# Block 0's queries and keys stored once, a bias product and three pieces of work moved in a float32 transformer layer

## The chip, the core and the metric

The kernel runs on one core of a Trainium2 chip. The metric is the time of one execution on the device in microseconds, lower is better. A core has five engines that each run their own instructions in order: PE (matrix products), DVE (vectors), ACT (activation functions), POOL (general, slower), and SP, which here only issues DMA transfers. Transfers issued from SP, ACT or POOL are carried out by the core's 16 DMA engines. Engines wait for one another by semaphores.

## The reference

The input is 4096 tokens of 256 features, in float32. The layer is a causal attention with 16 heads of 16 features, followed by a feed-forward part with three gated or Gelu layers, each with a residual and a normalization on both sides:

```python
h = _layernorm(x)
q, k, v = split(h @ w_attn + b_attn)            # 16 heads of 16
logits = einsum('bhqd,bhkd->bhqk', q, k) * 16 ** -0.5
out = softmax(where(causal, logits, -inf)) @ v
x = x + _layernorm(out @ w_proj + b_proj)
h = silu(_tlin(_layernorm(x), w1)) * _tlin(_layernorm(x), w2)
h = gelu(_tlin(gelu(_tlin(h, h1)), h2))
x = x + _layernorm(_tlin(h, w3))
```

`_tlin` is a product with a matrix of -1, 0 and 1 times a scale per output. The attention is the first two thirds of the time, and the change lies at its beginning.

## The kernel before, in words

**Blocks and groups.** Tokens are worked in 8 blocks of 512 (`QB`). For block `j` the queries of the block meet the keys of blocks 0 to `j`, four heads at a time (a group `g`; 4 groups of 4 heads). The pair (j, g) is an item; 32 items run one after the other.

[...]

**Where the halves go.** `features(j, s, c, engine)` makes queries or keys (`s`) of block `j` for eight heads (`c` is 0 or 1): a product on PE into one PSUM bank (`pk` or `pq`), an ACT copy with the bias (`full`), a cast to `hi` and a subtraction to `lo` on `engine`, and then stores to a scratch tensor `halves_of[s, j]` in DRAM (L513, L545 to L551). It has the shape [16 heads, 2, 2, 16 features, 512], and each half is stored twice, so that a store counts 8 heads x 16 features x 512 numbers on the DRAM side. `hi` goes out from SP, `lo` of blocks 0 and 1 from POOL. `full`, `hi` and `lo` have one buffer for keys and one for queries.

**Reading back.** `load_rows` (L554) reads two heads as one tile of 128 rows x 512 (256 KB) with one transfer from SP. `queries(j, g)` loads two such tiles into a pool of two buffers per tag, `keys(n, c)` two tiles for item `n` and key block `c`, into a ring of 16. Every item reads its keys anew, those of block 0 (`c = 0`) too.

**A score unit.** `SharedUnit.products` (L843) multiplies keys by queries into a [128, 2, 512] PSUM tile, `maximum` (L852) takes its largest value on DVE, and `finish` (L859) writes the exponential of it with a shift per block, on ACT; on the diagonal POOL sets entries to zero (L866). `Values.step` multiplies the exponentials by the values on PE (L930). `steps(j)` lists the units of an item: 8j + 5.

**The order of work.** All engines follow the order in which Python records the instructions. `prep(j)` is a generator that normalizes block `j`, transposes it (`pt`), calls `features` four times and makes the values (`pv`); each `yield` ends a piece. A `Background` holds such generators and takes pieces between score units: `even` runs at most one PE piece of one job per call, `step` one piece of the first job, `finish(name)` steps until that job is gone. `project(j)` is the output projection of a finished block, `halve_weights` stores rounded weights for the second part, and `norm_block` starts the second part.

**The opening** (L1115 to L1132). Both `prep(0)` and `prep(1)` run up to their first PE piece, so both blocks are normalized: block 0 by DVE, block 1 by POOL. Then `biases()` (L1102) scales the query bias on DVE and, on PE, multiplies the value bias by the projection (`pb`, L1106), to be added to the projection's bias `bp`. Then `prep(0)` runs until queries and keys of heads 0 to 7 are stored, items 0 and 1 have their queries and keys loaded from SP, `prep(0)` runs to its end, and the score loop begins with `prep(1)` as its background.

Of the kernel before, what the change touches and what calls it, by code (L numbers as in the profile page):

```python
# [10 lines left out]
F32 = mybir.dt.float32  # L11
F32R = mybir.dt.float32r
AF = mybir.ActivationFunctionType
ALU = mybir.AluOpType
# [3 lines left out]
P = 128  # L18
QB = 512
# [98 lines left out]
def sandwich_kernel(  # L118
# [35 lines left out]
    scratch = ctx.enter_context(  # L154
        tc.tile_pool(name="scratch", bufs=1, space=bass.MemoryType.DRAM)
    )
# [199 lines left out]
    def norm_block(j, room, done, early=None):  # L356

        if early is None:
            xb[j] = load_block(0, x1[j])
            for _ in range(3):  # L360
                yield True
        else:
            xb[j] = early
        xj = xb[j]
        mv = stat.tile([P, NT, 2], F32, tag="mv", name=f"mvf_{j}")
        for t in range(NT):
            layernorm_stats(xj[:, t, :], mv, t)
            yield True
        rstd = layernorm_rstd(mv)
        xh = room.tokens(j)  # L370
        for t in range(NT):
            normalize(xh[:, t, :], xj[:, t, :], mv, rstd, t)
        yield True
        if early is not None:
            yield True
        pts = room.banks(f"ptf_{j}")
        for c in range(DC):
            for t in range(NT):
                nc.tensor.transpose(
                    pts[c][:, t * P : (t + 1) * P], xh[:, t, c * P : (c + 1) * P], ident  # L380
                )
        done(pts)
        yield True
# [20 lines left out]
    def attention(shared):  # L404
# [8 lines left out]
        with ExitStack() as actx:  # L413
# [61 lines left out]
            def constants():  # L475
# [35 lines left out]


            halves_of = {  # L513
                (s, j): scratch.tile([H, 2, 2, HD, QB], F32, tag=f"{s}_{j}", name=f"{s}_{j}")
                for s in "kq"
                for j in range(NB)
            }
# [1 line left out]
            def features(j, s, c, engine):  # L519

                i = "qk".index(s)
                ps = room.bank(f"p{s}_{j}_{c}")
                for d in range(DC):
                    yield room.within(d)
                    nc.tensor.matmul(  # L525
                        ps,
                        lhsT=wqk[d][:, i * D + c * P : i * D + (c + 1) * P],
                        rhs=xTs[j][:, d, :],
                        start=(d == 0),
                        stop=(d == DC - 1),  # L530
                    )
                lent.append(True)
                full = piece(f"full{i}", f"full{s}_{j}_{c}")
                nc.scalar.activation(
                    full,
                    ps,
                    AF.Identity,
                    bias=bqk[:, i * DC + c : i * DC + c + 1],
                    scale=1.0 if i else SCALE,
                )  # L540
                hi = piece(f"hi{i}", f"hi{s}_{j}_{c}")
                engine.tensor_copy(hi.bitcast(F32R), full)
                lo = piece(f"lo{i}", f"lo{s}_{j}_{c}")
                engine.tensor_tensor(lo.bitcast(F32R), full, hi.bitcast(F32R), ALU.subtract)
                for half, part in enumerate((hi, lo)):  # L545
                    for d in range(2):
                        at = (d, half) if i else (half, d)
                        queue = nc.gpsimd if shared and j < 2 and half else nc.sync
                        queue.dma_start(
                            out=halves_of[s, j][8 * c : 8 * (c + 1), at[0], at[1]], in_=part  # L550
                        )  # L551
                stored.add((s, j, c))

            def load_rows(tag, name, key, j, h):  # L554

                t = (piece if key == "k" else query)(tag, name, F32R)
                nc.sync.dma_start(
                    out=t.bitcast(F32),
                    in_=halves_of[key, j][h : h + 2].rearrange("h a b d n -> (h a b d) n"),
                )  # L560
                return t

            def query(tag, name, dtype):
# [10 lines left out]
            RING = 2 * NB  # L574
            kT, asked = {}, [0]

            def keys(n, c):

                for pr in range(2):
                    kT[n, c, pr] = load_rows(  # L580
                        f"k{asked[0] % RING}_{pr}", f"k{n}_{c}_{pr}", "k", c, 4 * (n % G) + 2 * pr
                    )
                asked[0] += 1

# [515 lines left out]
            issued = now = 0  # L1100

            def biases():  # L1102
                nc.vector.tensor_scalar(bqk[:, 0:DC], bqk[:, 0:DC], SCALE, None, ALU.mult)
                ps = two_banks("pb")[:, 0, 0:D]
                for c in range(DC):
                    nc.tensor.matmul(  # L1106
                        ps,
                        lhsT=bv[:, c : c + 1].to_broadcast([P, P]),
                        rhs=wp[:, c, :],
                        start=(c == 0),  # L1110
                        stop=(c == DC - 1),
                    )
                nc.vector.tensor_tensor(bp, bp, ps, ALU.add)

            works = [prep(0, nc.vector), prep(1, nc.gpsimd)]  # L1115
            for work in works:
                while bg.piece(work) != Background.PE:
                    pass
            biases()
            while ("q", 0, 0) not in stored:  # L1120
                bg.piece(works[0])
            for n in range(2):
                queries(*items[n])
                keys(*chunks[n])
            while bg.piece(works[0]) is not False:
                pass
            if shared:
                bg.add(("prep", 1), works[1], PREP)
                bg.work[0][3] = Background.PE
            else:  # L1130
                while bg.piece(works[1]) is not False:
                    pass  # L1132
            mxs = {}
            for n, (j, g) in enumerate(items) if shared else ():
                if g == 0:
                    bg.finish(("prep", j))
                if g == G - 1 and j + 1 < NB:
                    while ("q", j + 1, DC - 1) not in stored:
                        bg.step()
                if n + 1 < len(items) and items[n + 1] not in qT:  # L1140
                    queries(*items[n + 1])
                if g == 0:
                    mxs[j] = top.tile([P, G * width(j)], F32, tag="mx", name=f"mx_{j}")
                    columns = iter(mxs[j][:, i : i + 1] for i in range(G * width(j)))
                if (j, g) == (NB - 2, G - 1):
                    for key in ("w1", "w2"):
                        W[key] = weight_pieces(key, TAGS[key])
                        load_pieces(rounded[key], W[key])
                if (j, g) == (NB - 1, G - 2):
                    for _ in halving:  # L1150
                        pass
                    bg.add(("norm", 0), norm_block(0, room, first_features), NORM)
                if (j, g) == (NB - 1, G - 1):
                    W["h1"] = weight_pieces("h1", TAGS["h1"])
                    load_pieces(rounded["h1"], W["h1"])
                for p, (shapes, parts) in enumerate(steps(j)):
                    ask(n, p)
                    if (g, p) == (1, 2) and j + 2 < NB:
                        bg.add(("prep", j + 2), prep(j + 2), PREP)
                    if (g, p) == (0, 2) and j:  # L1160
                        rise_of(j - 1, mxs[j - 1], f"rise_{j}")
                    units = [SharedUnit(j, g, f"{p}_{i}", at) for i, at in enumerate(shapes)]
                    for unit in units:
                        unit.products()
                        values.step(now)
                        now += 1
                        unit.maximum()
                        if n or p:
                            unit.finish()
                    if not n and not p:  # L1170
                        nc.vector.tensor_reduce(run[:, 0:1], mxs[0][:, 0:2], AX.X, ALU.max)
                        spread(run[:, 0:1], 0)
                        for unit in units:
                            unit.finish()
                    values.add(j, g, parts, [unit.e for unit in units], now - 1)
                    if j < 2 or p < NT * j:
                        bg.even(1 + j // 2 - j // 6)
                    if j > 0 and p % 4 == 2 and p < NT * j:
                        next(halving, None)
                if g == G - 2 and j + 1 < NB:  # L1180
                    next_shift(j)
# [326 lines left out]
```

## Time and profile before

| | us |
|---|---|
| median of 3 runs | 2053.32 (2049.60 to 2054.11) |
| the profiled execution | 2048.42 |
| its span in the profile | 2046.5 |
| busy in the span: PE, DVE, ACT, POOL | 1825.3, 1609.8, 1399.2, 552.2 |
| last exponential of the attention ends | 1375.6 |

A profile of one execution gives each instruction's start and length on its engine. The "chain of waits" follows the work that ended last back to the start: at each step to what released it. A line such as `72.14 8.13 DMA k<-k` in it says: from 72.14 us on, 8.13 us were spent waiting for a transfer that writes `k` (the tile) from `k` (the scratch tensor). In a table of windows each row is a stretch of time with every engine's busy time in it, PE's granted clock as a share of full speed, the mean busy share of the 16 DMA engines and what they moved in GB/s. SP's issues in the opening, from its timeline (start, length, line, transfer):

```profile
20.48 1.39 SPq L549 DMA_DIRECT2D k<-hik  x2
23.24 2.60 SPq L549 DMA_DIRECT2D q<-hiq  x2
33.79 0.84 SPq L557 DMA_DIRECT2D q<-q  x2
34.81 0.91 SPq L557 DMA_DIRECT2D k<-k  x2
35.76 0.95 SPq L557 DMA_DIRECT2D q<-q  x2
36.75 1.59 SPq L557 DMA_DIRECT2D k<-k  x2
```

Between 25.84 and 33.79 SP issued nothing: its next instruction loads queries, and they were not all stored yet.

### The profile page before, as it was taken

What the parts mean: (1) busy time and instruction counts of PE and PEld (TensorE: products, weight loads), DVE (VectorE), ACT (ScalarE), POOL (GpSimd) and SP (SyncE); (2) the same over time, 40 slices, a digit from 0 to 9 for tenths busy, and PEclk for the clock granted to TensorE, in tenths of its full rate; (3) what the DMA queues carried; (4) which work ended last, traced back from release to release, by engine and by line L of the source; (5) the groups of instructions that cost most, each with busy time, mean ns of one, the idle gap of its engine ahead of it and who ended that gap; (6) DMA issues with size and microseconds to landing.
All of it is one profiled execution on the core that took longest, in us unless ns stands there. A gap on an engine that the chain in (4) does not pass through costs nothing.

```text
span 2046.5 us, 28401 instructions
## 1 busy us (share of the span) xinstructions
PE 1825.3 (89%) x10518; PEld 932.5 (46%) x10518; DVE 1609.8 (79%) x1894; ACT 1399.2 (68%) x1598; POOL 552.2 (27%) x871
## 2 busy tenths in 40 slices
PE   4799989988888888888888887889999999999997
PEld 2333332322322322223222222228888888888886
DVE  3689998998999999999999999985546456465453
ACT  2699999999999999999999998982212222222221
POOL 3264545434435335333333110000120000000000
PEclk8899999999999999999999998999999999999999
DMA  6756645444235333553234213103100000000000
GB/s 168 229 179 219 191 133 180 147 154 159 98 131 183 116 103 124 161 163 115 76 136 156 98 44 101 63 9 114 53 11 21 15 7 21 1 21 21 1 11 15
DMA packets 134909, 202.09 MB, mean 99 GB/s; under 512 B 16064, under 2 KB 60736, under 8 KB 134752
## 3 DMA queue, kind: packets, MB, share of 16 engines
q1 hardware_dynamic: 130496, 194.56, 29.3%
q0 software_dynamic: 2480, 4.35, 1.0%
q8 instruction: 87, 1.43, 0.3%
q10 hardware_dynamic: 1776, 1.18, 0.3%
q14 instruction: 70, 0.57, 0.1%
HBM read 137.91 MB, written 62.13 MB: 98 GB/s over the span
## 4 chain that ended last, share of the span: by engine, by line
PE 46%; ACT 21%; DVE 19%; issue 6%; DMA 4%; POOL 2%; SPq 1%; ACTq 0%; POOLq 0%; DVEq 0%
PE z L1358 21%; ACT e_s L859 19%; DVE mx L852 18%; PE av L930 7%; PE s L843 7%; PE za L1358 3%; PE zb L1358 2%; PE pyf L1440 2%; DMA k<-k 1%; PE py L314 1%; PE pk L525 1%; PE pv L650 1%; PE pq L525 1%; ACT junk L211 1%; DMA q<-hiq 0%
## 5 line engine op out<-in xcount | busy, mean ns | idle before, releaser
L852 DVE TENSOR_REDUCE mx<-s 128x1 f32<-128x1024 f32 x1056 | 1219.8, 1217 | 72.1 <-PE s L843 66.6
L859 ACT ACTIVATE e_s<-s,shift 128x1024 f32<-128x1024 f32 x1056 | 1153.6, 1117 | 104.9 <-DVE mx L852 81.9
L843 PE MATMUL s<-q,k 64*128 64x512 f32 (+3 forms) x2304 | 517.7, 468 | 161.2 <-ACT e_s L859 144.7
L930 PE MATMUL av<-e_s,v 128*32 128x512 f32 (+2 forms) x4576 | 572.8, 575 | 7.9 <-POOL e_s L866 5.7
L843 PEld LDWEIGHTS s<-q,k 64*128 64x128 f32 x2304 | 208.9, 185 | 752.9 <-ACT e_s L859 652.2
L1425 ACT ACTIVATE fb<-z,sh 128x512 f32<-128x512 f32 x128 | 88.1, 689 | 364.8 <-PE z L1358 340.2
L1358 PE MATMUL z<-hb_0l,h 128*128 128x512 f32 x512 | 199.5, 390 | 0.0
L1358 PE MATMUL z<-hb_0h,h 128*128 128x512 f32 x512 | 199.5, 390 | 0.0
L866 POOL TENSOR_SCALAR_AFFINE_SELECT e_s<-e_s 128x256 f32<-128x256 f32 (+1 forms) x224 | 94.7, 440 | 337.4 <-ACT e_s L859 337.4
L233 POOL TENSOR_TENSOR rstd<-ve,neghalf 128x4 f32<-128x4 f32 (+1 forms) x22 | 20.8, 944 | 608.8 <-DVE ve L231 603.0
L930 PEld LDWEIGHTS av<-e_s,v 128*32 128x32 f32 x4576 | 97.2, 109 | 151.5 <-issue 116.1
L1325 DVE CAST hb_1h<-fb 128x512 fp32r<-128x512 f32 x64 | 27.4, 428 | 155.7 <-ACT fb L1425 155.7
L1402 ACT ACTIVATE sl<-za,s 128x512 f32<-128x512 f32 x64 | 44.0, 690 | 120.4 <-PE za L1358 60.9
L1325 DVE CAST hb_0h<-fb 128x512 fp32r<-128x512 f32 x64 | 28.1, 440 | 99.6 <-ACT fb L1425 99.6
L1358 PEld LDWEIGHTS z<-hb_0h,h 128*128 128x128 f32 x512 | 96.1, 188 | 20.0
L1358 PEld LDWEIGHTS z<-hb_0l,h 128*128 128x128 f32 x512 | 96.2, 188 | 19.8
L1011 POOL TENSOR_SCALAR wc<-wc 128x256 f32<-128x256 f32 x88 | 75.8, 861 | 7.8
L1010 POOL TENSOR_TENSOR wc<-wc,wh 128x256 f32<-128x256 f32 x88 | 64.3, 730 | 7.2
L1012 POOL TENSOR_TENSOR fit<-fit,wc 128x256 f32<-128x256 f32 x88 | 64.2, 730 | 7.3
L1009 POOL CAST wh<-wc 128x256 fp32r<-128x256 f32 x88 | 35.0, 397 | 108.4 <-DMA wc<-in_h_t_dram 75.9
L1440 PE MATMUL pyf<-w,hb_1l 128*128 128x256 f32 x256 | 61.8, 284 | 0.0
L1440 PE MATMUL pyf<-w,hb_1h 128*128 128x256 f32 x256 | 61.7, 283 | 0.0
(257 smaller groups left out, 1970.3 us busy)
## 6 DMA issues: line engine op xcount, KB each, us to landing
k<-k SPq DMA_DIRECT2D x288, 256.0 KB
q<-q SPq DMA_DIRECT2D x64, 256.0 KB
x<-in_x_dram SPq DMA_DIRECT2D x16, 512.0 KB
k<-hik SPq DMA_DIRECT2D x32, 256.0 KB
q<-hiq SPq DMA_DIRECT2D x32, 256.0 KB
wc<-in_h_t_dram SPq DMA_DIRECT2D x64, 128.0 KB
r_h<-wh SPq DMA_DIRECT2D x64, 128.0 KB
h<-r_h SPq DMA_DIRECT2D x32, 256.0 KB
```

What stands on the lines that cost most here:

```text
L843: nc.tensor.matmul(self.both[:, i, col : col + n], lhsT=kT[G * j + g, c, pr][r, tt * P : (tt + 1) * P], rhs=qT[j, g][pr][r, QB - n :], sta ...
L852: nc.vector.tensor_reduce(next(columns), self.both.rearrange("p a n -> p (a n)"), AX.X, ALU.max)
L859: nc.scalar.activation(e, self.both, AF.Exp, bias=shifts[j])
L866: nc.gpsimd.affine_select(out=here, in_=here, compare_op=ALU.is_ge, fill=0.0, base=0, pattern=[[0, here.shape[1]], [1, P]], channel_multip ...
L930: nc.tensor.matmul(self.av[h * HW : (h + 1) * HW, QB - n :], lhsT=vb[kt // NT][:, kt % NT, o : o + HW], rhs=of(es, h), start=(kt == 0 or k ...
L1010: nc.gpsimd.tensor_tensor(w, w, hi, ALU.subtract)
L1011: nc.gpsimd.tensor_scalar(w, w, 0.0, None, ALU.is_equal)
L1012: nc.gpsimd.tensor_tensor(fit, fit, w, ALU.mult)
L1325: nc.vector.tensor_copy(hi, full)
L1358: nc.tensor.matmul(ps, lhsT=w[c], rhs=single(part[:, c, :]), start=(c == 0 and i == 0), stop=(c == kc - 1 and i == parts - 1),)
L1425: nc.scalar.activation(h, z, AF.Gelu, scale=sc[:, oc : oc + 1])
L1440: nc.tensor.matmul(ps[:, 0:D], lhsT=single(part[:, c, t * P : (t + 1) * P]), rhs=(w3_r if halves else w3_sb)[:, c, :], start=(c == 0 and i ...
```

## The change

1. Block 0's scratch tensors keep each half once: `[16, 16, 2, 512]` for keys, `[16, 2, 16, 512]` for queries. For block 0 `features` issues one store per half, not two. Blocks 1 to 7 still store each half twice, with the last two of the small axes exchanged.
2. `load_rows` of block 0 reads each half twice: a query tile with one transfer whose source repeats each row, a key tile with two transfers (one head each), whose source repeats the head's 32 rows.
3. `keys` and `load_rows` take the queue to issue from. Item 0's keys are issued from POOL, all others from SP as before.
4. The bias product `pb` and its addition to `bp` stand behind the whole of `prep(0)`; the scaling of the query bias stays where it was.
5. Ahead of the score loop `prep(1)` is stepped until the keys of its heads 0 to 7 are stored: two transposes and one pass of `features`.
6. In item (7, 2) the background first finishes `project` of block 6, and then adds `norm_block`.

```diff
             halves_of = {
-                (s, j): scratch.tile([H, 2, 2, HD, QB], F32, tag=f"{s}_{j}", name=f"{s}_{j}")
+                (s, j): scratch.tile(
+                    [H, 2, HD, 2, QB] if j else [H, HD, 2, QB] if s == "k" else [H, 2, HD, QB],
+                    F32, tag=f"{s}_{j}", name=f"{s}_{j}",
+                )
...
                 for half, part in enumerate((hi, lo)):
-                    for d in range(2):
+                    queue = nc.gpsimd if shared and j < 2 and half else nc.sync
+                    kept = halves_of[s, j][8 * c : 8 * (c + 1)]
+                    for d in range(2) if j else ():
                         at = (d, half) if i else (half, d)
-                        queue = nc.gpsimd if shared and j < 2 and half else nc.sync
-                        queue.dma_start(
-                            out=halves_of[s, j][8 * c : 8 * (c + 1), at[0], at[1]], in_=part
-                        )
+                        queue.dma_start(out=kept[:, at[0], :, at[1]], in_=part)
+                    if not j:
+                        queue.dma_start(out=kept[:, :, half] if i else kept[:, half], in_=part)
                 stored.add((s, j, c))
-            def load_rows(tag, name, key, j, h):
+            def load_rows(tag, name, key, j, h, queue=nc.sync):
                 t = (piece if key == "k" else query)(tag, name, F32R)
-                nc.sync.dma_start(
-                    out=t.bitcast(F32),
-                    in_=halves_of[key, j][h : h + 2].rearrange("h a b d n -> (h a b d) n"),
-                )
+                to, part = t.bitcast(F32), halves_of[key, j][h : h + 2]
+                if j:
+                    queue.dma_start(out=to, in_=part.rearrange("h a d b n -> (h a d b) n"))
+                elif key == "k":
+                    for i in range(2):
+                        rows = part[i : i + 1].rearrange("u d b n -> u (d b) n")
+                        queue.dma_start(
+                            out=to[i * P // 2 : (i + 1) * P // 2],
+                            in_=rows.broadcast_to([2, 2 * HD, QB]),
+                        )
+                else:
+                    rows = part.rearrange("h a (d u) n -> (h a d) u n", u=1)
+                    queue.dma_start(out=to, in_=rows.broadcast_to([P // 2, 2, QB]))
                 return t
...
             def biases():
-                nc.vector.tensor_scalar(bqk[:, 0:DC], bqk[:, 0:DC], SCALE, None, ALU.mult)
                 ps = two_banks("pb")[:, 0, 0:D]
...
-            biases()
+            nc.vector.tensor_scalar(bqk[:, 0:DC], bqk[:, 0:DC], SCALE, None, ALU.mult)
             while ("q", 0, 0) not in stored:
                 bg.piece(works[0])
             for n in range(2):
                 queries(*items[n])
-                keys(*chunks[n])
+                keys(*chunks[n], nc.sync if n or not shared else nc.gpsimd)
             while bg.piece(works[0]) is not False:
                 pass
+            biases()
             if shared:
                 bg.add(("prep", 1), works[1], PREP)
                 bg.work[0][3] = Background.PE
+                while ("k", 1, 0) not in stored:
+                    bg.step()
...
                 if (j, g) == (NB - 1, G - 2):
                     for _ in halving:
                         pass
+                    bg.finish(("project", NB - 2))
                     bg.add(("norm", 0), norm_block(0, room, first_features), NORM)
```

More of the change, by code (lines that the diff above doesn't have):

```diff
@@ L513, in attention @@
             halves_of = {
-                (s, j): scratch.tile([H, 2, 2, HD, QB], F32, tag=f"{s}_{j}", name=f"{s}_{j}")
+                (s, j): scratch.tile(
+                    [H, 2, HD, 2, QB] if j else [H, HD, 2, QB] if s == "k" else [H, 2, HD, QB],
+                    F32,
+                    tag=f"{s}_{j}",
+                    name=f"{s}_{j}",
+                )
                 for s in "kq"
@@ L545, in features @@
                 for half, part in enumerate((hi, lo)):
-                    for d in range(2):
+                    queue = nc.gpsimd if shared and j < 2 and half else nc.sync
+                    kept = halves_of[s, j][8 * c : 8 * (c + 1)]
+                    for d in range(2) if j else ():
                         at = (d, half) if i else (half, d)
-                        queue = nc.gpsimd if shared and j < 2 and half else nc.sync
+                        queue.dma_start(out=kept[:, at[0], :, at[1]], in_=part)
+                    if not j:
+                        queue.dma_start(out=kept[:, :, half] if i else kept[:, half], in_=part)
+                stored.add((s, j, c))
+            def load_rows(tag, name, key, j, h, queue=nc.sync):
+                t = (piece if key == "k" else query)(tag, name, F32R)
+                to, part = t.bitcast(F32), halves_of[key, j][h : h + 2]
[4 more added lines that the diff above has]
+                        rows = part[i : i + 1].rearrange("u d b n -> u (d b) n")
                         queue.dma_start(
-                            out=halves_of[s, j][8 * c : 8 * (c + 1), at[0], at[1]], in_=part
-                        )
-                stored.add((s, j, c))
-            def load_rows(tag, name, key, j, h):
-                t = (piece if key == "k" else query)(tag, name, F32R)
-                nc.sync.dma_start(
-                    out=t.bitcast(F32),
-                    in_=halves_of[key, j][h : h + 2].rearrange("h a b d n -> (h a b d) n"),
-                )
+                            out=to[i * P // 2 : (i + 1) * P // 2],
+                            in_=rows.broadcast_to([2, 2 * HD, QB]),
+                        )
+                else:
+                    rows = part.rearrange("h a (d u) n -> (h a d) u n", u=1)
+                    queue.dma_start(out=to, in_=rows.broadcast_to([P // 2, 2, QB]))
                 return t
@@ L575, in attention, with keys @@
             kT, asked = {}, [0]
-            def keys(n, c):
+            def keys(n, c, queue=nc.sync):
                 for pr in range(2):
                     kT[n, c, pr] = load_rows(
-                        f"k{asked[0] % RING}_{pr}", f"k{n}_{c}_{pr}", "k", c, 4 * (n % G) + 2 * pr
+                        f"k{asked[0] % RING}_{pr}",
+                        f"k{n}_{c}_{pr}",
+                        "k",
+                        c,
+                        4 * (n % G) + 2 * pr,
+                        queue,
                     )
```

## The prediction

> **What bounds the kernel now.** I read the chain of waits first, then the groups of instructions by line, then the chain in order of time for the opening, and last short windows with the share of the DMA engines.
>
> The chain and the two costliest groups:
>
> ```profile
> PE 46%; ACT 21%; DVE 19%; issue 6%; DMA 4%; POOL 2%; SPq 1%; ACTq 0%; POOLq 0%; DVEq 0%
> L852 DVE TENSOR_REDUCE mx<-s 128x1 f32<-128x1024 f32 x1056 | 1219.8, 1217 | 72.1 <-PE s L843 66.6
> L859 ACT ACTIVATE e_s<-s,shift 128x1024 f32<-128x1024 f32 x1056 | 1153.6, 1117 | 104.9 <-DVE mx L852 81.9
> ```
>
> Until about 1380 us each of 1056 score units costs a maximum (1.22 us) and an exponential (1.12 us), side by side; after that PE is the bound. The change touches neither. DMA has only 4% of the chain, nearly all of it in the opening. The same chain in order of time:
>
> ```profile
> 23.86 9.77 DMA q<-hiq
> ...
> 35.21 5.63 DMA k<-k
> ...
> 72.14 8.13 DMA k<-k
> ...
> 81.53 10.63 DMA k<-k
> ```
>
> The first and second waits are block 0's stores and the read back, the third and fourth the keys of group 3 of block 0 and group 0 of block 1. The timeline of ACT and PE says what that costs:
>
> ```profile
> 31.10 2.00 PE L650 MATMUL pv<-wv,xT 128*128 128x256 f32 x8 [0.68 <-ACT v L658]
> 38.98 0.80 PE L843 MATMUL s<-q,k 64*128 64x512 f32 x2 [5.88 <-DMA k<-k]
> 44.42 2.12 ACT L859 ACTIVATE e_s<-s,shift 128x1024 f32<-128x1024 f32 x2 [10.70 <-DVE shift L1040]
> 94.16 2.24 ACT L859 ACTIVATE e_s<-s,shift 128x1024 f32<-128x1024 f32 x2 [1.87 <-DVE mx L852]
> 169.24 2.24 ACT L859 ACTIVATE e_s<-s,shift 128x1024 f32<-128x1024 f32 x2 [0.90 <-DVE mx L852]
> ```
>
> The last three are the first exponentials of blocks 0, 1 and 2. Block 0's four groups hold 4 x 5 units, some 35 us of work at the 8.9 us that a group took, but 49.7 us lie between the first two. So the opening has about 14 us of waiting; that is all a change here can win.
>
> Now the windows with the DMA share (before the last figure, which is GB/s):
>
> ```profile
> core 0: us, PE busy (x) PEld busy (x) DVE busy (x) ACT busy (x) POOL busy (x), PEclk, DMA share, GB/s
> 45.00:47.00 2.00, 1.38 (x8) 0.84 (x8) 1.32 (x2) 2.00 (x4) 0.81 (x2) 0.50 0.52 203
> 51.00:53.00 2.00, 2.00 (x4) 0.50 (x5) 0.00 (x0) 0.32 (x1) 0.63 (x1) 0.50 0.95 342
> 90.00:92.00 2.00, 1.26 (x6) 0.76 (x4) 0.00 (x0) 1.81 (x5) 0.87 (x3) 1.00 0.97 363
> 109.00:111.00 2.00, 1.49 (x20) 0.73 (x20) 2.00 (x3) 1.97 (x3) 1.58 (x5) 1.00 0.48 176
> ```
>
> In 51 to 53 and 90 to 92 only loads of whole 128-row tiles ran: all 16 engines busy. In 45 to 47 only stores of hik and hiq ran, whose DRAM side counts 8 heads x 16 x 512; in 109 to 111 mostly oo and xT0lo, whose DRAM side counts 8 x 16 x 512 too: half of the engines. So a transfer runs on no more engines than the outermost count of either side allows. Per busy engine the four windows give 22.5 to 24.4 GB/s; I use 23.4. Then 256 KB cost an engine 0.70 us over 16 engines and 1.40 us over 8.
>
> **The change part by part.** The bias product leaves the front: pb held PE from 12.37 to 14.42 waiting for wp, while block 0's tokens were normalized at 10.80 (9.42 + 1.38). So the transposes may start some 3.3 us sooner and the first hi store goes out at 17.2 instead of 20.48. The first lo store gains less: POOL still normalizes block 1 until 19.22 (14.38 + 4.84), so 19.3 instead of 21.48.
>
> The stores of block 0 fall from 16 to 8, 4 MB to 2 MB. Those of k now count 128 rows on both sides, so by the row they run on 16 engines. With one hi and one lo store each, hiq and loq land near 25.5 (issue near 20.7, then the 4 to 5 us that the first hik needed: 20.48 to 26.1 for two). The queries can be loaded then, not at 33.79: 8 us sooner.
>
> Three pieces of block 1 and pb stand ahead of the first scores on PE. With the rows' durations: second pv ends at 29.7, pb 31.7, pt 32.8, copy, pt 34.1, copy, pk 36.7. So the first scores run at 36.7, 2.3 us sooner, even if their keys lie ready at 30. The pieces aren't lost: block 0's own 12 steps have four PE pieces fewer to carry. What is queued behind them: DVE now has hik and lok of block 1 (0.43 + 0.69) ahead of the first maximum, and hik must wait until the store of block 0's second hik has landed (one buffer).
>
> The last edit (finishing project before norm) moves nothing: in the built order of instructions every engine's rows agree from block 5 on, but for the key loads. In blocks 1 to 4 the background stands one place later. I cost both at nothing; the cover is the maximum of 1.22 us per unit.
>
> Then the reading twice. Queries: 64 rows x 2, outermost counts 64 and 128: 0.70 us as before. Keys: each tile is now two transfers of 128 KB, with 64 rows on the SBUF side and **2 x 32 x 512 on the DRAM side, the 2 a repeat**. No row shows a count of 2. By what 8 does to stores and to loads alike, 2 means two engines: 64 KB each at 23.4 GB/s, 2.80 us per transfer, 11.2 us per group of four, on the same two engines if the choice always starts with the first. The other end is 8 or 16 engines: 0.35 to 0.70 us per transfer, 1.4 to 2.8 per group. I take two, since both kinds of row fell with the count. It holds for every group of every block but the very first, whose four go by POOL.
>
> [...]
>
> Those two engines get, until the keys of block 2's first group are there: block 0's keys for 8 groups, 8 x 11.2 = 89.6; other keys of block 1, 8 x 0.70 = 5.6; queries 18 x 0.70 = 12.6; SP's stores, block 0 4.2, block 1 8 x 1.40, block 2 16 x 1.40, together 37.8; POOL's 12 stores 0 to 16.8, taken as 8.4; 7 outputs 4.9; three x loads 4.2; oo and xT0lo 5.6; weights 2.1. Sum 170.8 us. From the first store at 17 that is 187.8; with 2.1 us for scores and maximum (0.8 + 1.24) block 2's first exponential comes at 190 against 169.24: **+21**. POOL's stores elsewhere: +12. Idle time of the two engines (about 5 us before the first keys, 6 us while SP waits for block 1's hiq) and POOL's stores on them: up to +40. I take the middle, **+26**. In block 2 the two engines get 11.2 + 2.8 + 1.4 + 5.6 + 1.4 + 0.7 + 0.7 + 3.5 = 27.3 us per group against 25.7 that a group took: 0 to +6, kept for the range. From block 3 on it is about 30 against 36 us: hidden, and 62 more issues of 0.45 us on SP lie beside 1200 us of scores.
>
> Span 2046.5 + 26 = 2072.5. The median of the runs, 2053.3, lies 6.8 above that span, so 2079.
>
> **The rivals.** *Spread (faster).* If key loads use 8 or more engines, or a changing pair, the first exponential comes at 42.3 (36.7 + 5.6 for two maxima, shift and block 1's casts) and block 1's at 42.3 + 4 x 8.9 + 3 x 1.5 = 82.4 instead of 94.16: -12, 2041; bounds -17 (no gaps) and -4 (half the gaps stay, with more to carry): 2036 to 2049. For it: there is no row with a count of 2, and the waits of 8.13 and 10.63 us are real. Against: the two halved windows.
>
> [...]
>
> *The jam spreads (far slower).* SP's queue is in order and each half has one buffer: behind a late store wait DVE's casts (block 1) or POOL's (block 2 on), and with them the maxima or the masks. If every group of blocks 0 to 2 loses 5 us more, +60: 2110.
>
> **How the numbers follow.** Two fixed engines 0.61 (own range 2061 to 2099), spread 0.24, hidden 0.08, jam 0.07. Faster or slower by over 0.2% (4 us, about what a measurement of this kernel can tell) follows from the same cases. Slower: 0.61 + 0.07 + 0.02 = 0.70; same 0.06 (hidden, less what falls outside 4 us); faster 0.24. The likeliest gives 2079. The range reaches down into the spread case to 2038 and up to 2100, and leaves out the jam and the best of the spread.
>
> **What would show it.** Right: windows with k<-k alone at a share near 0.13 and 45 to 50 GB/s; a first exponential of block 0 near 47 (hik of block 1 held by a store), of block 1 near 101 and of block 2 near 195; PE s waiting for k<-k 30 us or more in all; blocks 3 to 7 unchanged. Wrong: key loads landing within 4 us at a share near 1, block 1 starting before 85. The stores are right if the wait of 9.77 us for hiq is gone in either case.

## The result and the profile after

| | before | after |
|---|---|---|
| median of 4 runs, us | 2053.72 (2049.60 to 2055.87) | 2122.12 (2119.28 to 2124.76) |
| ratio to before, 95% interval | | 1.0335 (1.0312 to 1.0358) |
| span of the profiled execution | 2046.5 | 2117.5 |
| first exponential of block 0, 1, 2 | 44.42, 94.16, 169.24 | 54.77, 115.67, 210.91 |
| first exponential of block 3, last one's end | 276.25, 1375.6 | 334.82, 1447.6 |

The change made the kernel 3.35% slower. The prediction had the direction and the two slow DMA engines, but said 2079. The chain of waits of after, and the same two groups of instructions:

```profile
PE 44%; ACT 19%; DVE 16%; DMA 10%; issue 6%; SPq 3%; POOL 2%; ACTq 0%; POOLq 0%; DVEq 0%
L872 DVE TENSOR_REDUCE mx<-s 128x1 f32<-128x1024 f32 x1056 | 1220.1, 1215 | 112.2 <-PE s L863 108.3
L879 ACT ACTIVATE e_s<-s,shift 128x1024 f32<-128x1024 f32 x1056 | 1154.9, 1116 | 156.5 <-DVE mx L872 128.2
```

The busy times are those of before within 1.3 us (1219.8 and 1153.6). What grew is the third figure, the idle time ahead of them: 72 to 112 for the maxima, 105 to 157 for the exponentials. DMA went from 4% to 10% of the chain, and SP's own queue from 1% to 3%. So no work was added to the two engines that set the pace; they wait.

Some of SP's issues in the opening, and three windows in which hardly anything but block 0's keys was being read:

```profile
18.77 0.34 SPq L557 DMA_DIRECT2D k<-hik  x1
23.31 0.75 SPq L557 DMA_DIRECT2D q<-hiq  x1
30.85 2.65 SPq L575 DMA_DIRECT2D q<-q  x4
33.61 4.56 SPq L569 DMA_DIRECT2D k<-k  x4
38.27 2.35 SPq L557 DMA_DIRECT2D k<-hik  x1
```

```profile
39.00:41.00 2.00, 0.16 (x2) 0.00 (x0) 0.00 (x0) 0.28 (x1) 0.00 (x0) 1.00 0.13 51
45.00:49.00 4.00, 0.00 (x0) 0.00 (x0) 0.00 (x0) 0.00 (x0) 0.00 (x0) 0.50 0.13 50
117.00:122.00 5.00, 3.59 (x23) 1.36 (x27) 1.39 (x2) 1.45 (x3) 0.00 (x0) 0.57 0.13 49
```

A share of 0.13 is two engines of 16, at 49 to 51 GB/s. In 45 to 49 PE, DVE, ACT and POOL do nothing, and SP issues nothing between 41.36 and 50.40: all five stand still behind two busy DMA engines. The last line of the first fence says what they wait for. This store was issued at 38.27, after four key loads of 33.61 to 38.17. The chain in order of time shows that one and its like (start, length, what):

```profile
24.31 6.53 DMA q<-loq
...
38.27 11.59 DMA k<-hik
...
71.73 15.84 DMA k<-hik
...
103.66 14.70 DMA k<-k
...
124.20 10.70 DMA avd<-av_sb
...
152.88 11.77 DMA x<-in_x_dram
...
219.51 11.62 DMA avd<-av_sb
```

Only some of these are waits for the keys themselves. The others are a store of `hik`, the store of an attention output (`avd`) and a load of tokens (`x`). None of them belongs to block 0's reading, and each took 10 to 16 us (11.59 and 15.84, 10.70 and 11.62, 11.77). That they were late because they stood on SP behind key loads is so far a reading of the order of issue; experiments 4, 6 and 7 test it. What waits for the first `hik` store is on DVE:

```profile
49.95 0.43 DVE L547 CAST hik<-fullk 128x512 fp32r<-128x512 f32 x1 [15.47 <-DMA k<-hik]
```

This cast of block 1 waits for the buffer that the store of 38.27 empties. DVE runs in order, the first maximum is the instruction after next and starts at 51.02, and so the first exponential comes at 54.77.

### The profile page after: what moved, and what is told of

The parts are those of the page before. It is cut to its first block, busy times and chain, and to the rows that moved or that the text cites. A ratio compares the mean times of both kernels' runs of the same rounds, so it can differ in the third digit from the quotient of the medians.

```text
span 2117.5 us, 28458 instructions
## 1 busy us (share of the span) xinstructions
PE 1853.8 (88%) x10518; PEld 939.4 (44%) x10518; DVE 1612.2 (76%) x1894; ACT 1401.9 (66%) x1598; POOL 553.3 (26%) x871
## 4 chain that ended last, share of the span: by engine, by line
PE 44%; ACT 19%; DVE 16%; DMA 10%; issue 6%; SPq 3%; POOL 2%; ACTq 0%; POOLq 0%; DVEq 0%
PE z L1381 20%; ACT e_s L879 17%; DVE mx L872 14%; PE av L950 7%; PE s L863 6%; DMA avd<-av_sb 3%; PE za L1381 2%; PE zb L1381 2%; PE pyf L1463 2%; DMA k<-k 2%; DMA k<-hik 1%; PE py L314 1%; DMA x<-in_x_dram 1%; SPq L569 1%; SPq L565 1%
## 5 line engine op out<-in xcount | busy, mean ns | idle before, releaser
L863 PE MATMUL s<-q,k 64*128 64x512 f32 (+3 forms) x2304 | 527.2, 474 | 196.6 <-ACT e_s L879 163.1
L950 PE MATMUL av<-e_s,v 128*32 128x512 f32 (+2 forms) x4576 | 583.8, 586 | 7.5 <-POOL e_s L886 5.7
L1348 DVE CAST hb_1h<-fb 128x512 fp32r<-128x512 f32 x64 | 27.4, 427 | 155.7 <-ACT fb L1448 155.7
L1029 POOL CAST wh<-wc 128x256 fp32r<-128x256 f32 x88 | 35.0, 397 | 209.1 <-DMA wc<-in_h_t_dram 142.1
```

Source lines behind the costliest of these rows:

```text
L863: nc.tensor.matmul(self.both[:, i, col : col + n], lhsT=kT[G * j + g, c, pr][r, tt * P : (tt + 1) * P], rhs=qT[j, g][pr][r, QB - n :], sta ...
L950: nc.tensor.matmul(self.av[h * HW : (h + 1) * HW, QB - n :], lhsT=vb[kt // NT][:, kt % NT, o : o + HW], rhs=of(es, h), start=(kt == 0 or k ...
L1348: nc.vector.tensor_copy(hi, full)
```

## The experiments

All times are medians; the ratio to the kernel before, run on the same chip, stands with its 95% interval. Experiments 1 to 4, 5 to 8 and 9 to 12 ran on three chips; where two from different chips are compared, it is by these ratios.

**1. Reading with four 32-row transfers in place of two that repeat.** After, with each key tile of block 0 read by four transfers of 32 different rows:

```diff
-                    for i in range(2):
-                        rows = part[i : i + 1].rearrange("u d b n -> u (d b) n")
-                        queue.dma_start(
-                            out=to[i * P // 2 : (i + 1) * P // 2],
-                            in_=rows.broadcast_to([2, 2 * HD, QB]),
-                        )
+                    for i in range(4):
+                        rows = part[i // 2 : i // 2 + 1].rearrange("u d b n -> (u d b) n")
+                        queue.dma_start(out=to[i * 2 * HD : (i + 1) * 2 * HD], in_=rows)
```

> The changed kernel with one edit: a key tile of block 0 is loaded by four transfers of 32 rows, none with a repeated source, in place of two transfers of 64 rows whose source repeats 32 rows twice. Same rows in the same places, stores once as in the changed kernel. Theory (two engines): all of the loss comes from the key loads that run on two engines, so the share of 0.13 is gone, block 1 starts before 90, and the time is 2036 to 2049 (the spread case of the prediction). Rival (order): the moved bias product, the pieces ahead of the scores or the new layout cause the loss; then it stays above 2100. Rival (number of transfers): eight transfers per group instead of four hold up SP; then between 2060 and 2100.

2048.17 us, ratio 0.9979 (0.9966 to 0.9992). Same bytes, twice as many issues, and the whole loss is gone. The first exponentials of blocks 0 and 1 are these:

```profile
45.92 1.11 ACT L876 ACTIVATE e_s<-s,shift 128x1024 f32<-128x1024 f32 x1 [7.88 <-DVE shift L1057]
95.33 1.11 ACT L876 ACTIVATE e_s<-s,shift 128x1024 f32<-128x1024 f32 x1
```

So the repeat as the outermost count is the cause of the loss. But the rival *Spread*, whose case this is, had 42.3 and 82.4 here: without the two engines the change still doesn't win the 12 us that *Spread* named.

**2. Only the moved work.** Before, with its own stores and loads, and the bias product behind `prep(0)`, the three pieces ahead of the scores, and the last edit:

```diff
-            biases()
+            nc.vector.tensor_scalar(bqk[:, 0:DC], bqk[:, 0:DC], SCALE, None, ALU.mult)
...
+            biases()
             if shared:
...
+                while ("k", 1, 0) not in stored:
+                    bg.step()
...
+                    bg.finish(("project", NB - 2))
```

> The kernel before with the moved bias product, the pieces of block 1 ahead of the first scores and the finish of project, but with its own stores and loads. Theory (two engines): no loss; a little gain or none, 2044 to 2056, since block 0's stores still bound the first scores. Rival (order): above 2075.

2049.97 us, 0.9978 (0.9968 to 0.9988): as fast as experiment 1. Storing block 0 once, read well, adds nothing to the moved work. One line of DVE shows that the opening gains nothing, without any two-engine load:

```profile
46.57 0.43 DVE L542 CAST hik<-fullk 128x512 fp32r<-128x512 f32 x1 [11.71 <-DMA k<-hik]
```

The three pieces put block 1's cast ahead of the first maximum, and its buffer is still being stored. The first exponentials of blocks 0 and 2 come at 51.40 and 173.31, later than before (44.42 and 169.24), and the attention ends at 1377.14 (1375.6). So where the 0.2% comes from, this profile doesn't show.

**3. Only the stores and reads of the change.** After, with the bias product, the pieces and the queue of item 0's keys as before:

```diff
+            biases()
             while ("q", 0, 0) not in stored:
...
-                keys(*chunks[n], nc.sync if n or not shared else nc.gpsimd)
+                keys(*chunks[n])
...
-            biases()
             if shared:
...
-                while ("k", 1, 0) not in stored:
-                    bg.step()
```

> The changed kernel with the bias product back at the front, no pieces ahead of the first scores, and all keys issued from SP: the storing once and reading twice alone. Theory (two engines): loses what the whole change loses or more, 2105 to 2140. Rival (order): near 2053 or below.

2139.3 us, 1.0421 (1.0403 to 1.0438): slower than after itself. The loss belongs to the reading, and the moved work softens it.

**4. Two engines from block 3 on only.** Experiment 1, with the change's two-engine loads for items of block 3 and later (`late` is `n >= 3 * G`):

```diff
-                elif key == "k":
+                elif key == "k" and not late:
                     for i in range(4):
...
+                elif key == "k":
+                    for i in range(2):
+                        rows = part[i : i + 1].rearrange("u d b n -> u (d b) n")
+                        queue.dma_start(
+                            out=to[i * P // 2 : (i + 1) * P // 2],
+                            in_=rows.broadcast_to([2, 2 * HD, QB]),
+                        )
```

> As e1 for items of blocks 0 to 2, with the two-engine key loads from block 3 on (20 of 32 items). Tells where the loss arises. By the prediction's step the pair is hidden from block 3 on: the same as e1 within 4 us. By the trace of the changed kernel, which lies 58.6 us behind at block 3's start and 71 us behind at the end: e1 plus 8 to 16 us.

2061.78 us, 1.0041 (1.0027 to 1.0056): 0.62%, some 13 us, above experiment 1 (2048.17). The prediction had these loads hidden, since the two engines have about 30 us of work per group and a group takes 36 or more. The chain in order of time, between 440 and 700 us and between 700 and 1320:

```profile
612.37 12.01 DMA avd<-av_sb
624.39 2.26 DMA sums<-avd
...
635.93 5.65 DMA invd<-sums
...
642.86 7.96 DMA xT0lo<-invd
...
1089.75 10.80 DMA avd<-av_sb
...
1231.67 15.27 DMA x<-x
```

The keys themselves are nowhere in it: they arrive in time. Late are small transfers. Three of them (612.37, 1089.75 and 1231.67) were issued right behind four key loads, and others wait for the first of these (an output is stored, its sums are read, inverted, and read again). In experiment 1 the chain has no `avd` in these stretches: it holds 6.53 us of `x`, 7.35 us of `wc`, 2.58 us of `h`, and no other DMA wait above 2 us. No run moved only the small transfers of these blocks away from the key loads.

**5. Two engines in blocks 0 to 2 only.** The counterpart: after, with four 32-row transfers from block 3 on (`early` is `n < 3 * G`):

```diff
-                elif key == "k":
+                elif key == "k" and early:
                     for i in range(2):
...
+                elif key == "k":
+                    for i in range(4):
+                        rows = part[i // 2 : i // 2 + 1].rearrange("u d b n -> (u d b) n")
+                        queue.dma_start(out=to[i * 2 * HD : (i + 1) * 2 * HD], in_=rows)
```

> The changed kernel with its two-engine key loads kept for blocks 0 to 2, and four loads of 32 different rows per tile from block 3 on. Theory (the early and the late groups each lose their own time, and the losses add): after's 2122 less the 13.6 us that the late groups alone cost, 2108, between 2104 and 2112. Rival (the late groups lose because block 0 to 2 have left work over that they must catch up): the late loss goes in part, 2112 to 2120. Rival (the early loss hurts only as much as the pair's sum said, +26): 2080 or less.

2108.08 us, 1.0266 (1.0245 to 1.0288). Against experiment 1 the early groups cost 2.87%, 59 us, the late ones 13, and after 73 (3.56%): the two losses add up.

**6. The early loads from ACT's queue.** Experiment 5, with block 0's keys of items 1 to 11 issued from ACT:

```diff
-                        queue,
+                        nc.scalar if c == 0 and 0 < n < 3 * G else queue,
```

> As the run before it (two-engine key loads in blocks 0 to 2, four 32-row loads later), but those 44 early transfers of key block 0 are issued from ACT and not from SP. Same bytes, same number of engines by count, another queue. Theory (the loss is the in-order queue: small stores and loads of SP stand behind key loads, and the engines behind them): SP's avd, sums, x and hik transfers land within some 3 us again and at least half of the early loss of 60 us goes, 2080 or less, less up to some 20 us that ACT loses to the issues. Rival (the loss is the throughput of two engines): the same 2104 to 2112 or more, and k<-k still waited for as long.

2104.74 us, 1.0249 (1.0227 to 1.0271): hardly less. Waits between 30 and 280 us (total, times, longest):

```profile
ACT e_s L884 <- issue: 23.7, 3, 11.8
...
ACT e_s L884 <- DMA k<-lok: 10.1, 1, 10.1
ACT e_s L884 <- DMA k<-k: 7.2, 1, 7.2
```

The transfers of SP did come sooner: DVE's wait for `hik`, 14.6 us in experiment 5, is gone from the list, and that for `sums` fell from 10.5 to 3.9. But ACT, the engine of the exponentials, now stood 41 us (23.7, 10.1 and 7.2) at its own issues and their waits. And the chain between 61 and 121 us is now almost wholly key loads:

```profile
61.09 22.60 DMA k<-k
...
84.24 19.72 DMA k<-k
...
105.59 15.28 DMA k<-k
```

Block 2's first exponential came at 216.85, no sooner than in experiment 5 (214.35). So up to block 2 sooner small transfers gave nothing, half of the loss didn't go, and the time is the one that the rival named: there the work of the two engines itself holds the kernel. The loss moved to another queue; because ACT stood still too, the run doesn't separate queue from throughput cleanly.

**7. Half the dose.** Experiment 5, with one of the two heads of each tile read by two 32-row transfers, so that half as much runs on two engines:

```diff
-                    for i in range(2):
-                        rows = part[i : i + 1].rearrange("u d b n -> u (d b) n")
-                        queue.dma_start(
-                            out=to[i * P // 2 : (i + 1) * P // 2],
-                            in_=rows.broadcast_to([2, 2 * HD, QB]),
-                        )
+                    for i in range(2):
+                        rows = part[0:1].rearrange("u d b n -> (u d b) n")
+                        queue.dma_start(out=to[i * 2 * HD : (i + 1) * 2 * HD], in_=rows)
+                    rows = part[1:2].rearrange("u d b n -> u (d b) n")
+                    queue.dma_start(out=to[P // 2 : P], in_=rows.broadcast_to([2, 2 * HD, QB]))
```

> Two-engine loads for one of the two heads of each tile only, in blocks 0 to 2; the other head and all later groups by 32-row loads. The two engines' sum falls from 170.8 us by 45 to 126, well under the 169 us that block 2 took to come. Theory of the sum (throughput): nothing is left to wait for, 2046 to 2054. Theory of the queue (small transfers wait behind what is ahead of them): bursts of half the length still stand ahead of stores and loads, 10 to 35 us stay, 2058 to 2083.

2072.0 us, 1.0085 (1.0060 to 1.0111): 1.06% above experiment 1, 22 of the 59 us. By the sum of the two engines' work (126 us until block 2, which in before took 169) nothing should be left, yet block 2's first exponential came at 188.44, where experiment 1 has 170.85. The chain in order of time:

```profile
38.16 6.95 DMA k<-hik
...
73.36 12.49 DMA x<-in_x_dram
...
107.28 7.71 DMA avd<-av_sb
```

Small transfers are late here too, the stores of `hik` and `avd` by less than in experiment 5 (11.54 and 10.57). So a sum of work per stage isn't enough: these loads cost time although the sum left room.

**8. 128 rows on both sides everywhere.** The moved work of the change, but each half of every block stored by one transfer that repeats it on the SBUF side. The 64 rows of a head (16 features, `hi` and `lo`, each twice) are in the order feature, copy, half for keys and feature, half, copy for queries; a load is one transfer of 128 rows:

```diff
+                (s, j): scratch.tile([H, HD, 2, 2, QB], F32, tag=f"{s}_{j}", name=f"{s}_{j}")
...
+                    at = kept[:, :, :, half] if i else kept[:, :, half]
+                    twice = part.rearrange("p (u n) -> p u n", u=1).broadcast_to([P, 2, QB])
+                    queue.dma_start(out=at.rearrange("h d u n -> (h d) u n"), in_=twice)
...
+                queue.dma_start(out=to, in_=part.rearrange("h d a b n -> (h d a b) n"))
```

> The changed order of work, but for every block each half is stored by one transfer that repeats it on the SBUF side, into [16 heads, 16 features, 2, 2, 512], so that 128 rows are the outermost count of both sides of every store and every load, with one issue each. Theory (the outermost count sets the engines, for stores too): no window with stores at half share, and the time is at or below the 2048 of the four 32-row loads: 2038 to 2049. Rival (the stores' engines never mattered, since the first maximum waits for block 1's casts whatever they do): 2046 to 2052.

2034.63 us, 0.9904 (0.9880 to 0.9927): faster than both kernels. Its waits for DMA between 30 and 280 us are two lines, 8.0 us; before has eight, 32 us, and after nine, 92 us (waits of PE's products and weight loads for one transfer count twice in such a sum):

```profile
POOL wh L1016 <- DMA wc<-in_w_t_dram: 6.8, 2, 6.2
PE s L850 <- DMA k<-k: 1.2, 1, 1.2
```

```profile
46.20 1.11 ACT L866 ACTIVATE e_s<-s,shift 128x1024 f32<-128x1024 f32 x1 [4.85 <-DVE shift L1047]
84.75 1.14 ACT L866 ACTIVATE e_s<-s,shift 128x1024 f32<-128x1024 f32 x1
```

The first exponential of block 0 is no sooner than before, but block 1's comes at 84.75, not 94.16: block 0's groups follow one another without the waits. This kernel stores every half twice, as before did, so its gain doesn't come from fewer bytes. Its stores run on all engines (between 20.5 and 21.5 us, with only its first stores in flight, the DMA share was 1.02, where the stores of before had 0.52), and there are half as many of them, 512 KB each in place of 256 KB. No run separates these two; that experiment 1, with twice the key issues of after, lost nothing against experiment 2 speaks for the engines.

**9. The same layout alone.** The kernel before, with the stores and the load of experiment 8 and nothing moved:

```diff
-                    for d in range(2):
-                        at = (d, half) if i else (half, d)
-                        queue = nc.gpsimd if shared and j < 2 and half else nc.sync
-                        queue.dma_start(
-                            out=halves_of[s, j][8 * c : 8 * (c + 1), at[0], at[1]], in_=part
-                        )
+                    queue = nc.gpsimd if shared and j < 2 and half else nc.sync
+                    kept = halves_of[s, j][8 * c : 8 * (c + 1)]
+                    at = kept[:, :, :, half] if i else kept[:, :, half]
+                    twice = part.rearrange("p (u n) -> p u n", u=1).broadcast_to([P, 2, QB])
+                    queue.dma_start(out=at.rearrange("h d u n -> (h d) u n"), in_=twice)
```

> The kernel before, in its own order of work, with the layout of the stores that repeat each half on the SBUF side: [16 heads, 16 features, 2, 2, 512], one store per half, 128 rows as the outermost count everywhere; nothing else of the change. Theory (16 engines for the stores are the gain of the kernel that reached 2035, and the moved work is worth what it was worth alone, 4): 2037 to 2041. Rival (the two need each other: without block 1's keys ahead the waits of block 0's last group and block 1's first stay): 2045 to 2050.

2036.99 us, 0.9923 (0.9909 to 0.9936). The layout alone is 0.8%, nearly all of experiment 8.

**10 to 12. The moved parts, one at a time,** each taken out of experiment 8: the three pieces (10), the bias product put back to the front (11), the last edit (12).

```diff
-                while ("k", 1, 0) not in stored:
-                    bg.step()
```

> The 2035 us kernel without the three pieces of block 1 ahead of the first scores. Theory (the pieces hold the first maximum back: some 4.4 us of PE and 1.1 of DVE stand ahead of it): first exponential near 42 instead of 46.2, and the pieces then cost block 0's units less than that, 2030 to 2034. Rival (what goes ahead must be carried in block 0 anyway): 2034 to 2038.

```diff
+            biases()
             while ("q", 0, 0) not in stored:
...
-            biases()
             if shared:
```

> The 2035 us kernel with the bias product back at the front. The first transposes come some 4 us later (14.2 instead of 10.1). If PE runs its first products at 2.0 us then and not at 3.8, three products give 5.4 back: 2032 to 2035. If they run at 3.8 as they did where stores alone were changed: 2036 to 2039.

```diff
-                    bg.finish(("project", NB - 2))
```

> The 2035 us kernel without the last edit (project of block 6 no longer finished before norm is added). The prediction's price of nothing: 2032 to 2037, block 7 as long as before. Rival (that edit is the 4 us that the moved work gained alone): 2038 to 2040.

2033.77 (0.9913, 0.9899 to 0.9926), 2036.61 (0.9924, 0.9910 to 0.9937) and 2032.11 (0.9901, 0.9886 to 0.9916). None is told apart from experiment 8; that number 12 is the lowest of all proves nothing. Number 10 shows where a sooner start goes:

```profile
38.27 1.12 ACT L866 ACTIVATE e_s<-s,shift 128x1024 f32<-128x1024 f32 x1 [4.22 <-DVE shift L1047]
83.58 1.11 ACT L866 ACTIVATE e_s<-s,shift 128x1024 f32<-128x1024 f32 x1 [0.76 <-DVE mx L859]
```

Without the pieces the first exponential is 7.9 us sooner (38.27 against 46.20), but block 1 only 1.2 us: block 0's units now have the pieces between them.

## Why the prediction was right and wrong

**Right: what bounds, and the two engines.** The busy time of maxima and exponentials stayed, and windows with block 0's keys alone show a share of 0.13 and 49 to 51 GB/s, where 0.13 and 45 to 50 were named. That is 24.5 to 25.5 GB/s for each of the two, and the case that these loads stay hidden (0.08) didn't come. One sign fell short: between 30 and 280 us PE's products of the scores waited 22.4 us for `k<-k`, where 30 or more was named. The weight loads' 19.6 lie in the same stretches (at 78.23 a weight load had waited 3.51 and its product 3.00) and can't be added. Experiment 1 takes the two engines away and with them the whole loss.

**Too small: the idle time and POOL's stores, of which the middle was taken.** The sum for block 2's first exponential was +21, with POOL's stores and idle time up to +40, and "I take the middle, +26". It was +41.7 (169.24 to 210.91): the upper end. Block 1 was due near 101 and came at 115.67. The trace has at most one transfer record in flight for 16.6 us between 17 and 211 us, where 11 us of idle time were put in; 17, the sum of 170.8, these 16.6 and 2.1 for scores and maximum give 206.5. This bookkeeping fits two engines that are always at work, and so does experiment 6, in which block 2 came no sooner. But experiment 7 says that it isn't the cause alone: with the sum at 126, 22 us were still lost. The sum also puts all of SP's other transfers, and half of POOL's stores, on the two engines of the keys. No run shows which engines those took; after shows that the `hik` store issued at 38.27 landed at 49.86, while from 45 to 49 us the share was that of two engines (0.13).

**Wrong: "0 to +6" in block 2, and "from block 3 on ... hidden".** From block 2's to block 3's first exponential another 16.9 us were lost, where the sum of 2079 took 0, and after that some 12 (71.0 of the span less 41.7 and 16.9), where it took 0 too. With the 15.7 by which +26 was short, that is the 45 us between the predicted span of 2072.5 and 2117.5. Experiment 4 has the late part by itself: 13 us, with room on the two engines. The step that failed is the test that sets the work of the two engines per group against the length of a group. It asks whether the keys come in time, and from block 3 on they do. It doesn't ask how long a small transfer stands behind 11 us of key loads, and who waits for it. Block 2 shows it in one group: its first took 40.32 us (210.91 to 251.23) against 26.28 in before, which is 14.0 of the 16.9. In the chain of after stands there the `avd` store issued at 219.51 behind four key loads, with 11.62 us, and then 2.13 us for its `sums`. (The groups of block 2 took 26.1 to 27.4 us in before, not 25.7, so the test itself gave some 2 us and not 6.)

That was written down as the rival *The jam spreads*, priced at +60 (which makes 2113, not 2110) with a chance of 0.07, and as an either-or. It isn't one: late small transfers come with the two slow engines, and they belonged in the likeliest case. The rival named DVE's casts of block 1 rightly, but not POOL's casts of later blocks: between 300 and 1450 us those waited for ACT alone, 71.4 us against 91.7 in before. POOL's wait that grew is another, for the weights `wc`: 195.4 us there (142.1 and 53.3), where before has 94.0 (75.9 and 18.1) up to 1390.

**The opening.** First scores were due at 36.7 and came at 38.43; the first exponential was due at 47 and came at 54.77. The wait of the cast for its buffer was allowed some 5 us by that date (47 against the 42.3 without a wait); it took 15.47. Experiment 1 has the same stores and the same order without the two engines, and there this wait is half as long:

```profile
DVE hik L547 <- DMA k<-hik: 7.8, 1, 7.8
```

So about half of it comes with the two engines, and the rest, by the order of the instructions, with the three pieces. With the stores of before, experiment 2 has 11.71.

**The stores.** The wait of 9.77 us for `hiq` went, as named, but one of 6.53 us for `loq` took its place, and the queries were issued at 30.85, not 25.5. The front was to gain 3.3 us by moving the bias product, and the `hiq` store went out at 23.31, where before had 23.24. PE's first products ate it:

```profile
13.75 3.78 PE L530 MATMUL pk<-xT,wqk 128*128 128x512 f32 x4 [0.68 <-ACT xT L657]
18.31 3.78 PE L530 MATMUL pq<-xT,wqk 128*128 128x512 f32 x4 [0.78 <-ACT fullk L539]
22.87 1.98 PE L530 MATMUL pk<-xT,wqk 128*128 128x512 f32 x4 [0.78 <-ACT fullq L539]
```

In before all of them took 1.98 or 1.99. The prediction took its rows from there and had no term for it.

**No gain without the two engines.** *Spread* had 2041. Experiment 1 is 0.2% below before, 4 us, as much as the moved work alone. *Spread* counted 8.9 us for each group of block 0 and 1.5 between them; in experiment 1 the four groups take 49.4 us (45.92 to 95.33), and in experiment 8, with next to no waits, still 38.6. What neither the change nor *Spread* touches is the stores of blocks 1 to 7: experiment 9 gets 0.8% from the new layout of all stores, with the bytes and the order of before.

**Nothing for the last edit and for the issues on SP** holds: experiments 12 and 1 (twice as many issues as after, no loss).

## What to carry to other kernels

Write a transfer so that the outermost count of both sides is large: a repeat of 2 in front left 2 DMA engines of 16 here (a share of 0.13), and small transfers issued behind it came late (10 to 16 us in after), also where the total load looked harmless (7 to 12 us in experiment 7). When a transfer gets slower, do both: add up the work of a stage, and look for the small transfers issued behind it and for the in-order engine that needs them. Here either test alone fell short. Put the repeat on the side and at the place where it doesn't become the outermost count, here behind the 128 rows of SBUF (a share of 1.02 in experiment 8).

## What the runs showed that was not expected

**PE's first products at half speed, for a time that differs between the profiles.** Experiment 9 has the same order of work on PE as before, the bias product at 12.39 (before 12.37) and the transposes at 14.22 (14.21). Its first products:

```profile
17.75 3.78 PE L525 MATMUL pk<-xT,wqk 128*128 128x512 f32 x4 [0.68 <-ACT xT L636]
22.31 3.78 PE L525 MATMUL pq<-xT,wqk 128*128 128x512 f32 x4 [0.78 <-ACT fullk L534]
26.87 3.77 PE L525 MATMUL pk<-xT,wqk 128*128 128x512 f32 x4 [0.78 <-ACT fullq L534]
31.47 1.98 PE L525 MATMUL pq<-xT,wqk 128*128 128x512 f32 x4 [0.83 <-ACT fullk L534]
```

Three products at 3.78 us where before had none: 5.4 us. Experiments 1, 3, 4 and 12 had one such product, after and 10 two, 5, 7, 8 and 11 three, whether the bias product stood ahead or not; after and experiments 1, 5 and 7 have the same order on PE up to there. The granted clock of the windows read 1.00 in these stretches (14 to 17 and 19 to 22 us of after), so the durations have to be read, and that the clock is the reason isn't shown. In experiment 9 PE stayed slow from 17.75 to 30.64 us, with pauses of 0.78 us between the products. What sets the number of slow products isn't shown, and none of these profiles shows one kernel twice. From such rows the start of this kernel can't be predicted to within some 5 us.

**A repeat behind the outermost count kept all engines.** The stores of experiment 8 (a share of 1.02) read each SBUF row twice and move 512 KB with one issue. Between 17 us and block 2's first exponential, 5 to 8 transfer records are in flight for some 9 us, where before has some 28. What the repeat itself costs, no run shows.
